# Where the last batch of a grouped convolution is normalised, and the order of the work behind the last block

## The chip, the cores and the metric

The kernel runs on one core of a Trainium2 chip. Its time is the device time of one execution in microseconds (us): 2987.53 us is the median of three runs, which lie between 2986.3 and 2987.64 us. All data are float32.

## The reference, cut to what matters

The input `x` has shape (32, 14, 14, 512). Two layers follow each other; both add their result to their own input.

```
x = x + blocks(gn(x))            # layer 0
x = x + conv3x3(gn(x), W)        # layer 1: 32 groups of 16 channels, padding SAME

def gn(v):                       # for each image and each group of 16 channels
    return (v - mean) / sqrt(var + 1e-5)

def blocks(x):
    for i in range(18):
        nx = gelu(x @ block_w[i] + block_b[i])       # 512 x 512, for every pixel
        if i in (11, 14, 17):
            pooled = nx.mean over the pixels
            h = gelu(pooled @ fc1_w[t] + fc1_b[t])
            gates = softmax((h @ fc2_w[t] + fc2_b[t]).reshape(-1, 3, 512), axis=1)
            nx = nx + gammas[t] * (gates * anchors).sum()
        x = nx                                       # blocks 1, 4 and 9 are the anchors
    return x
```

What matters here is the second layer: a mean and a scale for each image and group have to be known before the convolution of that image can run on normalised data, while the addition at the end takes the data as they were.

## The kernel before, in words

**Pairs and blocks.** The 32 images are worked on in 8 pairs p of two tiles n, each tile with two images (392 pixels). Channels lie on the partitions, in four chunks c of 128. One `block` is one of the 18 multiplications for one pair, done by Strassen's scheme in seven products of eight matmuls (L390). There are 144 blocks and one empty step (GAP), 145 steps in an order written out in `steps`; the blocks of neighbouring pairs are interleaved.

**Ticks.** All other work is put into a calendar: seven ticks belong to each block, and `block` calls `run(tick)` after each product (after the copies or additions that belong to it). What stands in a tick is issued then, in the order in which it was put there, and each engine works through its own instructions in that order. `at` puts a function at a fixed tick; `put` looks for the first tick from a given one on that has room for its costs (`ROOM`, in us for VectorE as "dve" and ScalarE as "act"), and takes the room away; `hold` only takes room away. From `tend` = 7 x 145 = 1015 on there are no blocks, the room of a tick is `TAIL`, and the ticks give nothing but an order. In the text "tick +4" is `tend` + 4.

**Input.** `plan_start` loads each later pair's input in eight pieces of 98 pixels (`load_in`, L245, three buffers of `inpool`), turns each by four transposes (`turn_in`, L258), takes statistics and normalises, within the 35 ticks ahead of the pair's first block.

**End of a pair.** After block 17 `plan_head` and `plan_gates` issue the gates: `gate_hidden` (hps, L506), `gate_logits` (lps, L522), `gate_softmax`, and then for each chunk `gate_part` (L580), `gate_last` (L594, ScalarE) and `gate_add` (L602). A DMA of the POOL queue (`residual`, L666) adds layer 0's input to the result. `plan_norm` takes statistics (L196), brings them to scales (`scales_mean`, `scales_rstd`, `scales_newton`, the first two with a matmul, L203, that adds up the 16 partitions of a group), and writes each chunk to DRAM twice with `columns`: as it is (e=0, a copy by ScalarE, L680) and normalised (e=1, L692 by ScalarE, for the last pair L690 by VectorE). The DMAs are those of L699, two of 224 KB for each copy, in the tensor `x2d`.

**Convolution.** Two pairs make a batch m of 8 images, of which there are four. A batch has 16 units u, four for each chunk; a unit has two groups g. `unit_load` brings both copies (e=0 and e=1) into a tile `xs` by one DMA of 448 KB (L817) and, where they are not held, the weights as bands. In `xs` a partition holds one channel and column of the image, so the eight groups of a chunk lie side by side along the tile's free dimension, and no longer on partitions of their own. `unit_taps` runs 12 matmuls on e=1 (cps, L838), `unit_sum` adds the result to e=0 (L848), `unit_out` transposes (tpo, L862), copies (L867) and, after the fourth unit of a chunk, stores (L872). Batches 0 to 2 run beside the blocks of later pairs; the last six units of batch 2 and all of batch 3 (pairs 6 and 7) run behind the last block. PSUM has six buffers for products and units, and two for everything that is called `aux` (hps, lps, tpo, tpi, mps, vps).

**Start.** While the first scales are computed, 20 matmuls of constant data (`warm`, L950) run on TensorE. `load_gates` brings the gates' weights (L476, L481) at the block's tick 4.

Of the kernel before, what the change touches and what calls it, by code (L numbers as in the profile page):

```python
# [19 lines left out]
def kernel(  # L20
# [21 lines left out]
    P = 128  # L42
# [28 lines left out]
    fpool = ctx.enter_context(tc.tile_pool(name="fpool", bufs=1))  # L71
    qpool = ctx.enter_context(tc.tile_pool(name="qpool", bufs=38))
    tmp = ctx.enter_context(tc.tile_pool(name="tmp", bufs=6))
    inpool = ctx.enter_context(tc.tile_pool(name="inpool", bufs=3))
    outpool = ctx.enter_context(tc.tile_pool(name="outpool", bufs=2))
    cvpool = ctx.enter_context(tc.tile_pool(name="cvpool", bufs=2))
    small = ctx.enter_context(tc.tile_pool(name="small", bufs=2))
# [31 lines left out]


    ROOM = {"dve": (1.7, 0.0, 3.4, 3.4, 1.7, 0.0, 0.0), "act": (1.0, 0.8, 1.5, 1.5, 1.0, 0.8, 0.8)}
    TAIL = {"dve": 3.0, "act": 3.6}
    left = {e: {} for e in ROOM}

    def at(tick, fn, *args):
# [42 lines left out]
        mask[:, 1 : GP + 1], ident.rearrange("p (i k) -> p k i", k=GP), AX.X, ALU.add  # L158
    )

    mhalf = const.tile([P, NR], F32, name="mhalf")
    nc.vector.memset(mhalf, -0.5)

# [131 lines left out]
    def plan_start(p):  # L295

        t0 = NP7 * at_step[p, 0]
        parts = [(2 * p + n, s) for n in range(2) for s in range(TS)]
        NIN = 3
        a = t0 - LEAD  # L300
        turned = []
        for j, (t, s) in enumerate(parts):
            at(t0 - LEAD - 6 if j < NIN else turned[j - NIN], load_in, t, s)
            turned.append(put(max(a, turned[j - NIN] + 4 if j >= NIN else 0), {"act": 0.6}, turn_in, t, s))
            a = turned[j] + 1
        b = 0
        for n in range(2):
            for c in range(NCK):
                b = max(b, put(
                    turned[n * TS + TS - 1] + 1, {"dve": 1.0}, stats_in, 2 * p + n, c  # L310
                ))
        b = put(b + 1, {"dve": 0.8}, lambda: scales_mean(pst[p]))
        b = put(b + 1, {"dve": 0.2}, lambda: scales_rstd(pst[p]))
        b = put(b + 2, {"dve": 0.8}, lambda: scales_newton(pst[p]))
        e = b
        for c in range(NCK):
            e = max(e, put(b, {"dve": 1.6}, norm_in, p, c))
        b = e

        assert b < t0  # L320
        at(t0 - 1, take_start, p)
# [290 lines left out]
    def plan_head(p, i):  # L612

        k = at_step[p, i]
        t1 = NP7 * (k + 1)
        name = f"{p}_{i}"
        ti = TARGETS.index(i)
        box = boxes[p, i] = {}
        end = k == len(steps) - 1
        if p == 0:  # L620
            at(t1 + 1, gate_differences, k, ti)
        at(t1 + (0 if end else 1), gate_hidden, k, ti, name, box)
        box["base"] = {
            (h, n): put(t1, {"dve": 1.0}, gate_base, p, i, h, n) for h in range(2) for n in range(2)
        }
        a = t1 + (1 if end else 2)
        while room("dve", a) < 2.2:
            a += 1
        at(a, gate_logits, k, name, box)
        return put(a, {"dve": 2.2}, gate_softmax, ti, name, box)  # L630
# [40 lines left out]
    def columns(p, c, n, d, e, images=range(NI)):  # L671


        nx = boxes[p, NB - 1]["nx"]
        if n == 0 and 0 in images:
            d[e, c] = qpool.tile([P, W, PV], F32, tag="q", name=f"xc{e}_{p}_{c}")
        xc = d[e, c]
        src = nx[c // NH][n][:, c % NH, :].rearrange("p (b w h) -> p w b h", w=W, h=H)
        if e == 0:
            nc.scalar.copy(  # L680
                xc[:, :, n * NI * H : (n + 1) * NI * H].rearrange("p w (b h) -> p w b h", h=H), src
            )
        else:
            for b in images:
                q0 = (n * NI + b) * H
                r = c * NB4 + n * NI + b
                o, i = xc[:, :, q0 : q0 + H], src[:, :, b]
                scale, bias = d["mr"][:, 1, r : r + 1], d["mr"][:, 2, r : r + 1]
                if p == NPAIR - 1:
                    nc.vector.tensor_scalar(o, i, scale, bias, ALU.mult, ALU.add)  # L690
                else:
                    nc.scalar.activation(o, i, AF.Identity, scale=scale, bias=bias)  # L692
        if n == 0 or NI - 1 not in images:
            return
        del d[e, c]
        m, j = divmod(p, BP)
        for v in range(2):
            w0 = v * (W - KC)
            nc.sync.dma_start(  # L699
                x2d[m][c].rearrange("(q k) e v n -> q k e v n", k=KC)[  # L700
                    :, :, e, v, j * PV : (j + 1) * PV
                ],
                xc[:, w0 : w0 + KC],
            )

    def plan_norm(p, d, a, chunks):

        def stats(n, c, b):  # L710
            if "st" not in d:
                d.update(stats_tiles(f"b{p}"))
            stats_of(d, boxes[p, NB - 1]["nx"][c // NH][n][:, c % NH], c, n, (b,))

        last = a
        for c in chunks:
            for n in range(2):
                for b in range(NI):
                    last = max(last, put(a, {"dve": 0.36}, stats, n, c, b))
        r = chunks[0] * NB4, (chunks[-1] + 1) * NB4  # L720
        b = put(last + 1, {"dve": 0.8}, lambda: scales_mean(d, *r))
        b = put(b + 1, {"dve": 0.2}, lambda: scales_rstd(d, *r))
        b = put(b + 2, {"dve": 0.8}, lambda: scales_newton(d, *r))
        b += 1
        for c in chunks:
            for n in range(2):
                a = put(a, {"act": 0.6}, columns, p, c, n, d, 0)
        out = []
        for c in chunks:
            for n in range(2):  # L730
                for i in range(NI):
                    need = {"dve": 0.4} if p == NPAIR - 1 else {"act": 0.5}
                    b = put(b, need, columns, p, c, n, d, 1, (i,))
            out.append(b)
        return out

    def plan_end(p):
# [75 lines left out]
    def unit_load(m, u):  # L813

        c, ul = divmod(u, UC)
        xs = cvpool.tile([P, 2, 2, 2 * NV], F32, tag="x", name=f"x_{m}_{u}", bufs=NX)
        nc.sync.dma_start(  # L817
            xs.rearrange("r g e n -> r g (e n)"),
            x2d[m][c].rearrange("(g r) e v n -> r g (e v n)", r=P)[:, 2 * ul : 2 * ul + 2],
        )  # L820
        if u in bands:
            bw = bands[u] if m < NBAT - 1 else bands.pop(u)
        else:
# [2 lines left out]
                bw.rearrange("p g y d -> p (g y d)"), band[u].rearrange("p g n -> p (g n)")  # L826
            )
        units[m, u] = {"xs": xs, "bw": bw}

    def unit_taps(m, u):  # L830
        d = units[m, u]
# [46 lines left out]

    done = []

    def plan_unit(m, u, tk, ahead, stay=False):
        b = tk - ahead
        if not stay and len(done) >= NBW:
            b = max(b, done[-NBW][0])
        if len(done) >= NX:
            b = max(b, done[-NX][1])
        at(b, unit_load, m, u)
        a = max(b + 2, tk)
        while room("dve", a + 1) < 0.65:
            a += 1  # L890
        at(a, unit_taps, m, u)
        b = put(a + 1, {"dve": 0.65}, unit_sum, m, u)
        b = put(b + 1, {"act": 0.9}, unit_out, m, u)
        done.append((a, b))

    def plan_batch(m):


        ready = [max(ended[p][c] for p in range(m * BP, (m + 1) * BP)) for c in range(NCK)]
        if m < NBAT - 1:  # L900
            t0 = ready[-1] + 6
            t1 = ended[(m + 2) * BP - 1][-1] if m < NBAT - 2 else NP7 * at_step[NPAIR - 1, GAP] - 9
            early = NU - (NLATE + NGAP if m == NBAT - 2 else 0)
            for u in range(early):
                plan_unit(m, u, t0 + (t1 - t0) * u // early, 8)
            if m == NBAT - 2:
# [5 lines left out]
                        at(tk - 10, load_bands, (early + j,))  # L912
                    plan_unit(m, early + j, tk, 10, j >= NBW)
                for j in range(NLATE):
                    left["dve"][tend + 1 + j] += 0.65
                    left["act"][tend + 2 + j] += 0.9
                    at(tend - 12 + j, load_bands, (early + NGAP + j,))
                    plan_unit(m, early + NGAP + j, tend + j, 12, True)
        else:
            at(tend - 7, load_bands, (0, 1), wpool, "w", [P, NCK, C])  # L920
            for j in range(2):
# [1 line left out]
            at(tend + 1, load_bands, (4, 5), wpool, "w", [P, NCK, C])  # L923
            tk = 0
            for u in range(NU):
                tk = max(tk + 1, ready[u // UC] + 3, tend + NLATE)
                plan_unit(m, u, tk, 3, True)


    for s in range(TS):  # L930
# [15 lines left out]
    turn_biases(brow)  # L946

    warm = aux("warm")
    for j in range(20):
        nc.tensor.matmul(warm[:, :P], lhsT=ident, rhs=gmask, start=True, stop=True)  # L950
    scales_newton(pst[0])
    for c in range(NCK):
# [8 lines left out]
    for k in range(len(steps)):  # L961
# [9 lines left out]
            if p == 0:  # L971
                left["dve"][NP7 * (k - 1) + 4] = 0.0
        if i in TARGETS:
            at(NP7 * k + 4, load_gates, k)
            for tk, us in enumerate((0.8, 0.0, 1.5, 1.5, 0.5, 0.0, 0.0)):
                left["act"][NP7 * k + tk] = us
    for j in range(NLATE):
        left["dve"][tend + 1 + j] = TAIL["dve"] - 0.65
        left["act"][tend + 2 + j] = TAIL["act"] - 1.05
    for j in range(NLATE):  # L980
        left["dve"][tend + 1 + j] = TAIL["dve"] - 0.65
        left["act"][tend + 2 + j] = TAIL["act"] - 0.9
    left["act"][tend] = left["act"][tend + 1] = 0.0
    for j in range(NGAP):
        tk = NP7 * at_step[NPAIR - 1, GAP] + NP7 * j // NGAP
        hold("dve", tk + 1, 0.65)
# [15 lines left out]
    for g in range(C // CG):  # L1002
# [2 lines left out]
            b += 3  # L1005
        for dx in range(3):
            b = put(b, {"dve": 1.15 if dx else 0.6}, build_band, g, dx)
    assert b < ended[1][0]
    for m in range(NBAT):
        plan_batch(m)  # L1010
    for k in range(len(steps)):
# [35 lines left out]
```

## Time and profile before

The profiled execution took 2990.11 us; its span, from the first instruction to the last, is 2988.3 us. TensorE is at work in 2945.5 us of it and VectorE in 1734.0 us.

| stretch of the span | us | what runs |
|---|---|---|
| 0 to 22.04 | 22.0 | input, statistics and scales of pair 0, warm matmuls |
| 22.04 to 2882.06 | 2860.0 | the 144 blocks, with all else beside them |
| 2882.06 to 2926.0 | 43.9 | gates of pair 7, six units of batch 2, scales of pair 7 |
| 2926.0 to 2936.22 | 10.2 | TensorE without work |
| 2936.22 to 2981.26 | 45.0 | the 16 units of batch 3 |
| 2981.26 to 2988.3 | 7.0 | last copies and the last store |

The page's second part divides the span into 40 slices of 74.7 us; the rows of its chain of waits say what the end was waiting for at each moment, and the rows of an engine's waits what ended its idle time. In the rows of windows the columns are the stretch, its length, the busy time of TensorE, its weight load, VectorE, ScalarE and POOL with the number of instructions, and then the granted clock of TensorE (1.00 is full, 0.50 half), the share of the DMA engines and what they moved in GB/s.

### The profile page before, as it was taken

The page shows a single profiled execution, that of the slowest core. Times are in us where ns is not written, and L with a number is a line of the kernel's source. Part 1 is how long each engine was busy: PE and PEld are TensorE (multiplying, and loading weights), DVE is VectorE, ACT ScalarE, POOL GpSimd, SP SyncE. Part 2 cuts the span into 40 slices and gives each one's busy share as a digit, 9 for nine tenths or more (in the row PEclk, how much of TensorE's full clock was granted, in tenths as well). Part 3 has the DMA queues.
Part 4 walks back from the last instruction along what each step waited for, and adds up shares of the span by engine and source line. Part 5 has one row for each costly group of instructions (what it writes and reads, how often), then busy time and mean ns, then how long its engine had stood idle before and what let it go on. Part 6 is the DMA issues. An engine that isn't in the chain of part 4 may idle for free.

```text
span 2988.3 us, 31804 instructions
## 1 busy us (share of the span) xinstructions
PE 2945.5 (99%) x10113; PEld 1812.9 (61%) x10113; DVE 1734.0 (58%) x3309; ACT 1457.6 (49%) x3467; POOL 77.8 (3%) x60
## 2 busy tenths in 40 slices
PE   8999999999999999999999999999999999999986
PEld 5555555555566566666666666666666665656666
DVE  6877786655467454673546635565455653545663
ACT  4445445545455444554545544445445554544551
POOL 0000000000000000000000000000000000000010
PEclk9999999999999999999999999999999999999997
DMA  4444436633365345553455544555445653343678
GB/s 159 154 165 139 162 125 191 178 115 116 126 195 156 129 142 162 185 159 132 146 164 174 173 133 133 173 166 173 139 132 168 173 161 121 124 135 118 206 220 210
DMA packets 385743, 465.36 MB, mean 156 GB/s; under 512 B 150715, under 2 KB 213290, under 8 KB 385578
## 3 DMA queue, kind: packets, MB, share of 16 engines
q1 hardware_dynamic: 355178, 436.85, 46.4%
q0 software_dynamic: 4608, 12.85, 2.5%
q10 hardware_dynamic: 25792, 13.65, 1.7%
q8 instruction: 81, 1.33, 0.2%
q14 instruction: 84, 0.69, 0.1%
HBM read 381.48 MB, written 81.79 MB: 155 GB/s over the span
## 4 chain that ended last, share of the span: by engine, by line
PE 98%; DMA 1%; DVE 1%; issue 0%; ACT 0%; SPq 0%; DVEq 0%
PE x L390 51%; PE z L390 25%; PE y L390 13%; PE cps L838 5%; PE lps L522 1%; PE tpo L862 1%; PE tpi L258 1%; PE hps L506 1%; DMA tw<-in_L_conv_W_dram 0%; DMA w<-in_L_conv_fc_w_dram 0%; PE warm L950 0%; DMA w<-in_L_conv_block_w_dram 0%; DMA x2d<-xc 0%; PE mps_b L203 0%; DMA x<-x2d 0%
## 5 line engine op out<-in xcount | busy, mean ns | idle before, releaser
L390 PE MATMUL x<-t,s 128*128 128x392 f32 x2304 | 810.0, 494 | 0.0
L403 ACT ACTIVATE o<-c,bias 128x392 f32<-128x392 f32 x720 | 440.7, 620 | 663.0 <-DVE c L427 658.3
L390 PEld LDWEIGHTS x<-t,s 128*128 128x128 f32 x2304 | 432.5, 190 | 297.5
L427 DVE TENSOR_TENSOR c<-x,c 128x392 f32<-128x392 f32 x288 | 160.8, 565 | 515.5 <-PE x L390 423.8
L423 ACT COPY c<-x 128x392 f32<-128x392 f32 x576 | 278.4, 483 | 352.6 <-PE x L390 347.7
L390 PE MATMUL x<-t,w 128*128 128x392 f32 x1152 | 403.1, 493 | 0.9 <-DVE c L427 0.9
L390 PE MATMUL z<-t,s 128*128 128x392 f32 x1152 | 403.1, 493 | 0.0
L390 PE MATMUL z<-o,s 128*128 128x392 f32 x1088 | 380.9, 493 | 0.0
L390 PE MATMUL y<-o,w 128*128 128x392 f32 x1088 | 380.5, 492 | 0.0
L390 PE MATMUL x<-o,w 128*128 128x392 f32 x1088 | 380.3, 492 | 0.0
L427 DVE TENSOR_TENSOR c<-y,c 128x392 f32<-128x392 f32 x288 | 162.9, 566 | 294.3 <-PE y L390 206.7
L390 PEld LDWEIGHTS x<-t,w 128*128 128x128 f32 x1152 | 217.8, 190 | 157.9 <-DVE c L427 1.5
L390 PEld LDWEIGHTS z<-t,s 128*128 128x128 f32 x1152 | 217.0, 190 | 152.2
L369 DVE TENSOR_TENSOR t<-o,o 128x784 f32<-128x784 f32 x272 | 264.1, 971 | 65.4 <-ACT o L403 63.5
L390 PEld LDWEIGHTS x<-o,w 128*128 128x128 f32 x1088 | 206.4, 190 | 147.2
L390 PEld LDWEIGHTS y<-o,w 128*128 128x128 f32 x1088 | 205.1, 190 | 145.6
L390 PEld LDWEIGHTS z<-o,s 128*128 128x128 f32 x1088 | 205.0, 190 | 145.3
L369 DVE TENSOR_TENSOR t<-o,t 128x784 f32<-128x784 f32 x272 | 264.2, 971 | 4.7
L423 ACT COPY c<-z 128x392 f32<-128x392 f32 x288 | 139.2, 483 | 206.3 <-PE z L390 206.2
L427 DVE TENSOR_TENSOR c<-z,c 128x392 f32<-128x392 f32 x288 | 159.1, 563 | 118.8 <-PE z L390 118.0
L410 ACT ACTIVATE o<-c,bias 128x196 f32<-128x196 f32 x288 | 129.4, 450 | 91.0 <-DVE c L427 90.2
L403 ACT ACTIVATE o<-x,bias 128x392 f32<-128x392 f32 x240 | 137.5, 582 | 72.8 <-PE x L390 67.0
(107 smaller groups left out, 2061.2 us busy)
## 6 DMA issues: line engine op xcount, KB each, us to landing
w<-in_L_conv_block_w_dram SPq DMA_DIRECT2D x144, 1024.0 KB
s<-skeep SPq DMA_DIRECT2D x504, 256.0 KB
x2d<-xc SPq DMA_DIRECT2D x128, 224.0 KB
x<-x2d SPq DMA_DIRECT2D x64, 448.0 KB
skeep<-s SPq DMA_DIRECT2D x72, 256.0 KB
bw<-band SPq DMA_DIRECT2D x38, 384.0 KB
xkeep<-xt SPq DMA_DIRECT2D x32, 392.0 KB
o<-xkeep POOLq DMA_DIRECT2D x32, 392.0 KB, 7.6
```

The costliest lines, as they stand in the source:

```text
L258: nc.tensor.transpose(tp[:, c * TP : (c + 1) * TP], xs[:, c * P : (c + 1) * P], ident[:TP, :TP])
L369: nc.vector.tensor_tensor(t[j], i0, i1, ALU.subtract)
L390: nc.tensor.matmul(acc[d][:, :N], lhsT=lhsT[:, kk, d * P : (d + 1) * P], rhs=rhs[:, kk, :], start=first and kk == 0, stop=kk == NH - 1, sk ...
L403: nc.scalar.activation(o[:, d, :], srcs[d], AF.Gelu_apprx_tanh, bias=bias[:, r : r + 1])
L410: nc.scalar.activation(o[:, d, sl], srcs[d][:, sl], AF.Gelu_apprx_tanh, bias=bias[:, r : r + 1], accum_out=pooled[:, c, m : m + 1],)
L423: nc.scalar.copy(cs[d], acc[d][:, :N])
L427: nc.vector.tensor_tensor(cs[d], acc[d][:, :N], cs[d], ALU.add)
L506: nc.tensor.matmul(hps[:, :NB4], lhsT=w1[:, kk, :], rhs=box["pooled"][:, kk, :], start=(kk == 0), stop=(kk == NCK - 1),)
L522: nc.tensor.matmul(lps[:, m * NB4 : (m + 1) * NB4], lhsT=w2[:, m * P : (m + 1) * P], rhs=h, start=True, stop=True,)
L838: nc.tensor.matmul(pv[:, :, lo:hi], lhsT=d["bw"][:, g, dy], rhs=xv[:, :, lo + dy - 1 : hi + dy - 1], start=j == 0, stop=j == 2, skip_group ...
L862: nc.tensor.transpose(tp[:NV, j * P : (j + 1) * P], d["xs"][:, g, 0, v * NV : (v + 1) * NV], ident)
```

## The change

1. For pairs 6 and 7 `plan_norm` no longer calls `columns` with e=1. In its place a new function, `spread_scales`, multiplies the chunk's means and scales by a mask, so that each partition keeps its own group's value in its own column, and adds up over all partitions by a matmul with a matrix of ones (`ones`, new); ScalarE copies the result to the tile `spread`. Every partition then has the values of all eight groups of the chunk.
2. `unit_load` brings only e=0 for batch 3 (224 KB), and the new `unit_norm` makes e=1 from it in `xs`: for each of the two groups a subtraction and a multiplication on VectorE.
3. The units behind the last block get fixed ticks (`fixed`): taps two ticks apart, the sum one tick after the taps, the transposes three ticks after them, which is behind the next unit's taps. In batch 3 `unit_norm` stands one tick ahead of its taps, which is the tick of the sum of the unit before; `plan_unit` puts it there after that sum.
4. The last gates' steps have fixed ticks as well (logits +1, softmax +3, gates from +4 on); `scales_mean`, `scales_rstd` and `scales_newton` of all pairs are no longer moved to a tick with room, and the copies of e=1 of pairs 0 to 5 follow earlier. `TAIL` falls to 1.5 and 1.7.
5. `load_gates` of the last block moves from the block's tick 4 to its tick 1.
6. `inpool` has two buffers in place of three; a piece of the input is loaded when the piece two before it is turned, and turned at least three ticks later (before: three pieces and four ticks).
7. 16 warm matmuls in place of 20.

```diff
+    ones = const.tile([P, P], F32, name="ones")
+    nc.vector.memset(ones, 1.0)
...
-        NIN = 3
+        NIN = 2
...
-            turned.append(put(max(a, turned[j - NIN] + 4 if j >= NIN else 0), {"act": 0.6}, turn_in, t, s))
+            turned.append(put(max(a, turned[j - NIN] + 3 if j >= NIN else 0), {"act": 0.6}, turn_in, t, s))
...
+        if end:
+            at(t1 + 1, gate_logits, k, name, box)
+            at(t1 + 3, gate_softmax, ti, name, box)
+            return t1 + 4
...
+    spread = const.tile([P, NCK, GP, 2, BI], F32, name="spread")
+
+    def spread_scales(p, c, d):
+        shape = [P, GP, 2, NB4]
+        own = small.tile(shape, F32, tag="own", name=f"own_{p}_{c}")
+        nc.vector.tensor_tensor(
+            own, d["mr"][:, 0:2, c * NB4 : (c + 1) * NB4].unsqueeze(1).to_broadcast(shape),
+            ident[:, ::CG].unsqueeze(2).unsqueeze(3).to_broadcast(shape), ALU.mult,
+        )
+        ps = aux(f"sps_{p}_{c}")
+        n = GP * 2 * NB4
+        nc.tensor.matmul(
+            ps[:, :n], lhsT=ones, rhs=own.rearrange("p g v b -> p (g v b)"), start=True, stop=True
+        )
+        j = p % BP
+        nc.scalar.copy(
+            spread[:, c, :, :, j * NB4 : (j + 1) * NB4],
+            ps[:, :n].rearrange("p (g v b) -> p g v b", v=2, b=NB4),
+        )
...
+        b = last + 1
+        for us, fn, step in (
+            (0.8, scales_mean, 1), (0.2, scales_rstd, 2), (0.8, scales_newton, 1)
+        ):
+            hold("dve", b, us)
+            at(b, fn, d, *r)
+            b += step
+        late = p >= NPAIR - BP
...
+            if late:
+                b = put(b, {"dve": 0.2, "act": 0.25}, spread_scales, p, c, d)
+                out.append((a, b))
...
+        ne = 4 * NV if m < NBAT - 1 else 2 * NV
+        nc.sync.dma_start(xs.rearrange("r g e n -> r g (e n)")[:, :, :ne], src[:, :, :ne])
...
+    def unit_norm(m, u):
+        xs = units[m, u]["xs"]
+        c, ul = divmod(u, UC)
+        shape = [P, 2, BI, H]
+        for g in range(2):
+            o, i = [xs[:, g, e].rearrange("p (v b h) -> p v b h", v=2, h=H) for e in (1, 0)]
+            for v, op in ((0, ALU.subtract), (1, ALU.mult)):
+                w = spread[:, c, 2 * ul + g, v].unsqueeze(1).unsqueeze(3).to_broadcast(shape)
+                nc.vector.tensor_tensor(o, i if v == 0 else o, w, op)
...
+        if fixed:
+            b = a + 3
+            if m == NBAT - 1:
+                at(a - 1, unit_norm, m, u)
+            at(a + 1, unit_sum, m, u)
+            at(b, unit_out, m, u)
...
-                    plan_unit(m, early + NGAP + j, tend + j, 12, True)
+                    plan_unit(m, early + NGAP + j, tend + 2 * j, 12 + j, True, True)
...
-                tk = max(tk + 1, ready[u // UC] + 3, tend + NLATE)
-                plan_unit(m, u, tk, 3, True)
+                a, b = ready[u // UC]
+                tk = max(tk + 2, a + 4, b + 2, tend + 2 * NLATE)
+                plan_unit(m, u, tk, min(6, tk - a - 1), True, True)
...
-    for j in range(20):
+    for j in range(16):
...
-            at(NP7 * k + 4, load_gates, k)
+            at(NP7 * k + (1 if k == len(steps) - 1 else 4), load_gates, k)
```

More of the change, by code (lines that the diff above doesn't have):

```diff
@@ L73 @@
     tmp = ctx.enter_context(tc.tile_pool(name="tmp", bufs=6))
-    inpool = ctx.enter_context(tc.tile_pool(name="inpool", bufs=3))
+    inpool = ctx.enter_context(tc.tile_pool(name="inpool", bufs=2))
     outpool = ctx.enter_context(tc.tile_pool(name="outpool", bufs=2))
@@ L111 @@
     ROOM = {"dve": (1.7, 0.0, 3.4, 3.4, 1.7, 0.0, 0.0), "act": (1.0, 0.8, 1.5, 1.5, 1.0, 0.8, 0.8)}
-    TAIL = {"dve": 3.0, "act": 3.6}
+    TAIL = {"dve": 1.5, "act": 1.7}
     left = {e: {} for e in ROOM}
@@ L625, in plan_head @@
         }
-        a = t1 + (1 if end else 2)
+        if end:
+            at(t1 + 1, gate_logits, k, name, box)
+            at(t1 + 3, gate_softmax, ti, name, box)
+            return t1 + 4
+        a = t1 + 2
         while room("dve", a) < 2.2:
@@ L688, in columns @@
                 scale, bias = d["mr"][:, 1, r : r + 1], d["mr"][:, 2, r : r + 1]
[L689 to L692, printed above, removed]
+                nc.scalar.activation(o, i, AF.Identity, scale=scale, bias=bias)
         if n == 0 or NI - 1 not in images:
@@ L720, in plan_norm @@
         r = chunks[0] * NB4, (chunks[-1] + 1) * NB4
[L721 to L724, printed above, removed]
+        b = last + 1
[6 more added lines that the diff above has]
+        late = p >= NPAIR - BP
+        out = []
         for c in chunks:
@@ L727, in plan_norm @@
                 a = put(a, {"act": 0.6}, columns, p, c, n, d, 0)
-        out = []
-        for c in chunks:
+            if late:
+                b = put(b, {"dve": 0.2, "act": 0.25}, spread_scales, p, c, d)
+                out.append((a, b))
+        for c in chunks if not late else ():
             for n in range(2):
                 for i in range(NI):
-                    need = {"dve": 0.4} if p == NPAIR - 1 else {"act": 0.5}
-                    b = put(b, need, columns, p, c, n, d, 1, (i,))
-            out.append(b)
+                    b = put(b, {"act": 0.5}, columns, p, c, n, d, 1, (i,))
+            out.append((a, b))
         return out
@@ L816, in unit_load @@
         xs = cvpool.tile([P, 2, 2, 2 * NV], F32, tag="x", name=f"x_{m}_{u}", bufs=NX)
[L817 to L820, printed above, removed]
+        src = x2d[m][c].rearrange("(g r) e v n -> r g (e v n)", r=P)[:, 2 * ul : 2 * ul + 2]
+        ne = 4 * NV if m < NBAT - 1 else 2 * NV
+        nc.sync.dma_start(xs.rearrange("r g e n -> r g (e n)")[:, :, :ne], src[:, :, :ne])
         if u in bands:
@@ L879, with plan_unit @@
     done = []
-    def plan_unit(m, u, tk, ahead, stay=False):
+    def plan_unit(m, u, tk, ahead, stay=False, fixed=False):
         b = tk - ahead
@@ L888, in plan_unit @@
         a = max(b + 2, tk)
-        while room("dve", a + 1) < 0.65:
+        while not fixed and room("dve", a + 1) < 0.65:
             a += 1
         at(a, unit_taps, m, u)
-        b = put(a + 1, {"dve": 0.65}, unit_sum, m, u)
-        b = put(b + 1, {"act": 0.9}, unit_out, m, u)
+        if fixed:
[4 more added lines that the diff above has]
+            at(b, unit_out, m, u)
+        else:
+            b = put(a + 1, {"dve": 0.65}, unit_sum, m, u)
+            b = put(b + 1, {"act": 0.9}, unit_out, m, u)
         done.append((a, b))
     def plan_batch(m):
-        ready = [max(ended[p][c] for p in range(m * BP, (m + 1) * BP)) for c in range(NCK)]
+        ready = [
+            [max(ended[p][c][v] for p in range(m * BP, (m + 1) * BP)) for v in range(2)]
+            for c in range(NCK)
+        ]
         if m < NBAT - 1:
-            t0 = ready[-1] + 6
-            t1 = ended[(m + 2) * BP - 1][-1] if m < NBAT - 2 else NP7 * at_step[NPAIR - 1, GAP] - 9
+            t0 = ready[-1][1] + 6
+            t1 = ended[(m + 2) * BP - 1][-1][1] if m < NBAT - 2 else NP7 * at_step[NPAIR - 1, GAP] - 9
             early = NU - (NLATE + NGAP if m == NBAT - 2 else 0)
@@ L914, in plan_batch @@
                 for j in range(NLATE):
-                    left["dve"][tend + 1 + j] += 0.65
-                    left["act"][tend + 2 + j] += 0.9
                     at(tend - 12 + j, load_bands, (early + NGAP + j,))
-                    plan_unit(m, early + NGAP + j, tend + j, 12, True)
+                    plan_unit(m, early + NGAP + j, tend + 2 * j, 12 + j, True, True)
         else:
@@ L977 @@
     for j in range(NLATE):
[L978 to L983, printed above, removed]
+        hold("dve", tend + 2 * j + 1, 0.65)
+        hold("act", tend + 2 * j + 3, 0.9)
+    hold("dve", tend, -0.6)
+    hold("dve", tend + 1, -0.3)
+    hold("dve", tend + 3, 0.85)
+    for tick in range(tend, tend + 4):
+        hold("act", tick, room("act", tick))
     for j in range(NGAP):
@@ L1007 @@
             b = put(b, {"dve": 1.15 if dx else 0.6}, build_band, g, dx)
-    assert b < ended[1][0]
+    assert b < ended[1][0][1]
     for m in range(NBAT):
```

## The prediction

> **What bounds the kernel now.** The page first, then TensorE's waits: where it works without a break, only what adds to TensorE's own work can cost, and where it waits, the change can win.
>
> ```profile
> span 2988.3 us, 31804 instructions
> PE 2945.5 (99%) x10113; PEld 1812.9 (61%) x10113; DVE 1734.0 (58%) x3309; ACT 1457.6 (49%) x3467; POOL 77.8 (3%) x60
> ...
> PE cps L838 <- DMA x<-x2d: 10.2, 1, 10.2
> PE hps L506 <- DMA w<-in_L_conv_fc_w_dram: 5.5, 1, 5.5
> ...
> PE mps_b L203 <- DVE e_b L227: 3.5, 1, 3.5
> PE vps_b L203 <- DVE dv_b L216: 3.1, 2, 2.1
> ```
>
> All of these but 4.3 us of first input and one wait of 0.9 us near 56 us lie behind 2882.06, where the last block ends. The blocks are bound by TensorE, the tail of 106.2 us by what TensorE waits for. The chain of waits shows the largest gap and the last units:
>
> ```profile
> 2927.23 5.11 DMA x2d<-xc
> 2932.36 0.04 issue
> 2932.41 3.77 DMA x<-x2d
> 2936.17 0.04 issue
> 2936.22 4.57 PE cps L838 x12
> ...
> 2941.12 2.27 PE cps L838 x12
> ...
> 2977.66 2.18 PE cps L838 x12
> 2979.87 0.63 DVE x L848
> 2980.50 0.14 issue
> 2980.63 0.63 PE tpo L862 x4
> ```
>
> Normalised data go to DRAM (5.11) and come back (3.77); then come 16 units at 2.17 + 0.44 = 2.61 us (taps, transposes), of which the first is cold (4.57). From the last tap to the end of the span it is 8.5 us, before and after.
>
> **Start.** In the rows of `warm` the matmuls are at full speed from about 18.6 on, with some 11.5 passes in a us. Four matmuls fewer are 8 passes, 0.70 us. The first product then waits some 0.1 for VectorE's first four normalising steps (L284: 2.43 for 8 from 20.38, so until 21.63). Gain **0.6**. Bounds 0 and 0.7.
>
> **The blocks.** TensorE's work stays; the question is new waits.
> - Input with two buffers: at 515 to 525 us a piece was issued at 519.78 behind 1024 KB of weights and two stores of 392 KB; the windows there move all these bytes by 523.5. By the new ticks that place in SP's queue holds a piece turned after the third product, near 526.5: 3 us to spare. For pair 1 the piece is issued at 170.52 behind 1.5 MB moving at 350 GB/s, has landed by 174 and is turned at 175.3. I take 0. Bounds: 0, and 2 us for each of 7 pairs, 14.
> - Scales at fixed ticks: `scales_mean` comes two ticks earlier, behind the y product; VectorE's statistics end at 538.5 there, y at 540.8. `put` keeps finding room for all other VectorE work, and the moved tap loads (4 ticks ahead of their use in place of 5; 16 issues took 6.25 us) cost VectorE about 1 us, while a stall of 7.4 us cost TensorE 0.9. 0; bounds 0 and 1.
>
> **The tail up to the first unit of batch 3**, on the clock of this trace. `load_gates` moves in SP's queue ahead of the four stores of 2875.5 to 2880.8, so to about 2876; its weights came 5.2 us after their issue, so they are there by 2883.1, when pooled is (L410 ends at 2883.0). The stores behind it are needed 30 us later. hps 0.79, taps 2.17, lps 1.70, softmax 2.6 (as from 2897.28): the gates are ready at **2890.4**, before at 2899.96. Now something else is late: `residual`.
>
> ```profile
> L666 POOL DMA_DIRECT2D o<-xkeep x4: 844/921/997, 2881.6 to 2885.3; - x4
> DMA to landing us min/median/max: 6.2/9.9/11.8
> ```
>
> `gate_part` needs it. `scales_newton` of pair 6 (1.0 us) now stands ahead of `gate_base`, so the first two are issued near 2882.2 and 2883.1; with 9.9 the third `gate_part` starts at 2893.0 (bounds 2890.4 and 2895). Queued behind it on VectorE is the product of `spread_scales` for pair 6, and behind that one's matmul on TensorE the taps of unit 12: taps at 2893.8, a gap of almost 4 us since unit 11, with four transposes in it. Units 12 to 15 take 4 x 2.17 + 3 x 0.44 + 0.7 for mean and variance + 0.5 of handovers = 11.2, until 2905.0, cold taps and transposes 2.9 more: 2907.9. VectorE then works off 4.4 us (sum, newton 1.0, an addition, five statistics and parts, three products of `spread_scales`), until 2912.3. The e=0 columns are stored from 2904.3; with 5.1 to land and 3 for half the load (estimate from 3.77) they are there at 2912.5. **First taps at 2913.5**, 22.7 us before 2936.2. So the 10.2 us wait is gone, and 3.6 MB of stores and as much loading with it.
>
> **The 16 units.** `unit_norm` has no row. Its nearest is a multiplication with a repeated operand:
>
> ```profile
> L787 DVE TENSOR_TENSOR bt<-tw,mask x96: 541/552/560, 53.8 to 462.2; 128x384 f32<-128x384 f32 x96
> ```
>
> For 784 and 392 elements without repeats the next one starts after 0.89 and 0.48, which is 1.05 ns per element; 384 repeated fit that line. 224 elements: next start after 0.30, end after 0.385, a dependent one after 0.415. Four make 1.44. That VectorE has 2.0 us a unit and TensorE 2.61 hides nothing: in their tick the sum of unit u stands first and waits for the taps of u, the norm of u+1 comes behind it, and the taps of u+1 wait for that. Whether they wait for both groups is seen from two instructions that write one tile:
>
> ```profile
> 2808.92 0.81 ACT L594 ACTIVATE gq<-o,g 128x196 f32<-128x196 f32 x2
> ...
> 2809.76 0.57 DVE L602 TENSOR_TENSOR o<-o,gq 128x392 f32<-128x392 f32 x1 [2.11 <-ACT gq L594]
> ```
>
> ScalarE goes on with the other half of gq; the addition starts after its own two. So the taps wait for the first group alone: 0.03 + sum 0.53 + 0.415 + 0.385 + 0.14 = 1.50 behind the last tap, and with 2.17 a unit takes **3.67** in place of 2.61. Six of the 15 steps carry more VectorE work in between. The second: variance 0.35, its step 0.1, three parts 1.0, sum 0.53, norm 1.44, addition 0.48, statistics 0.54, product 0.2, handover 0.14, spreading 0.2, taps 2.17: 7.15. The next five, added up in the same way, 4.7, 5.2, 4.1, 4.7 and 4.7. Sum 30.5 + 9 x 3.67 = **63.5** from last tap to last tap.
>
> [...] Row first:
>
> ```profile
> 2882.00:2886.00 4.00, 0.06 (x1) 1.00 1.05 205
> 2886.00:2890.00 4.00, 2.47 (x10) 0.50 1.04 301
> ...
> 2938.00:2942.00 4.00, 4.00 (x19) 0.68 1.19 292
> ```
>
> The columns are TensorE's busy time, then its clock. After less than 4 us without work the clock is at half; from 2936.22 it takes 4.4 us of taps without a break to return (0.68 is 64% at half). [...] So unit 12, the first unit of batch 3 (6 us behind unit 15) and the second (5 us behind the first, waiting as listed) are cold. [...] I take the row: 2.4 more. [...]
>
> **The sum.** First taps 2913.5, cold 4.57: 2918.1; 63.5: 2981.6; two cold units 4.8: 2986.4; end 8.5: 2994.9; start -0.6: 2994.3, against a span of 2988.3. The execution of 2990.11 is 2.6 above the median of the runs; the difference of +6.0 is laid on the median: **2993.5**. The 22.7 us won ahead of the units are spent in them: 15 x 1.06 = 15.9 for the turn through VectorE, 7.9 for other VectorE work in it, 4.8 for the clock.
>
> **Rivals.**
> - Clock holds: units 12, the second and the third warm. -7.7: 2985.8. For it: no gap is longer than 6 us. Against it: the row of 0.50.
> - Faster: `unit_norm` lies behind the taps of the unit before, as its 2.0 against 2.61 us would allow, and the clock holds: a further 9 x 1.06 = 9.5 off, 2976.3. It decides if VectorE comes to the norm before the sum. Against it: the order inside the tick.
> - Clock stays at half: with 1.5 us of pause in each unit it doesn't return, or falls again. 13 units x 2.4 = 31 more: 3024.7; every other unit: 3009. For it: 2914 to 2926 at 0.50 with a busy share under a half. Against it: a cold unit is busy for 4.57 of 6.1 us.
> - Input late: 1 to 2 us for each of seven pairs, 3000.5 to 3007.5. Against it: 1.3 and 3 us to spare.
>
> **How the numbers follow.** Forecast 0.45 (its own range 2988 to 3001), clock holds 0.12, faster 0.13, half clock 0.22, input 0.08. A measurement tells 0.2%, 6 us, from no change; the forecast lies on that bound, 0.26 slower and 0.19 same. Slower 0.26 + 0.22 + 0.08 = 0.56; same 0.19 + 0.09; faster 0.13 + 0.03. The range 2978 to 3015 leaves out the end of the half clock and the faster end.
>
> **What would show it.** Right: the last units 3.7 us apart with TensorE waiting for VectorE (x, L848's tile); taps of 4.57 at the first units of batch 3; no wait of tpi for input. Wrong: units 2.61 apart; gates waiting for nothing at 2890; the clock at 0.50 beyond the third unit; first taps of batch 3 after 2918 or before 2909.

## The result, and the profile after

The changed kernel takes **2997.0 us**, the median of 11 runs (2994.24 to 2998.76), beside 2989.42 us for the kernel before on the same chip (11 runs, 2986.3 to 2994.88). The ratio is 1.0023, with a 95% interval from 1.0013 to 1.0032: the change costs a little. The profiled execution took 2994.24 us.

Line numbers are now those of the changed kernel, some 40 higher in the convolution: taps L878, `unit_sum` L888, `unit_norm` L868, the product of `spread_scales` L715 and its matmul L721, transposes L902, `gate_part` L582. The page of the changed kernel begins:

```profile
span 2992.5 us, 31865 instructions
PE 2950.6 (99%) x10121; PEld 1815.9 (61%) x10121; DVE 1752.8 (59%) x3366; ACT 1451.1 (48%) x3459; POOL 78.2 (3%) x60
```

VectorE has 18.8 us more work than before and TensorE 5.1; the span is 4.2 longer. TensorE's waits (total, times, longest, in us) tell which work it is that counts:

```profile
PE cps L878 <- DVE x L868: 11.6, 12, 1.0
PE sps L721 <- DVE own L715: 8.4, 6, 2.3
PE sps L721 <- DVE e_b L229: 4.5, 1, 4.5
```

The waits for x2d (10.2), for the gates' weights (5.5) are gone, and those of mps_b and vps_b (3.5 and 3.1) are no longer among the long ones. In their place stand twelve waits of about 1 us for `unit_norm`, and waits for the spreading of scales. Where this puts the end is seen in four stretches (us, from the starts and ends of TensorE's rows):

| stretch | before | after | difference |
|---|---|---|---|
| to the end of the blocks | 2882.06 | 2880.96 | -1.1 |
| end of the blocks to the first taps of batch 3 | 54.2 | 27.9 | -26.3 |
| first taps of batch 3 to the end of the last taps | 43.6 | 75.2 | +31.6 |
| last taps to the end of the span | 8.5 | 8.4 | -0.1 |

So the tail begins 26 us sooner and is 32 us slower. The chain of waits (start, duration) shows the steady turn of the last units, and further up what held the first unit behind the gates:

```profile
2882.30 8.30 DMA o<-xkeep
...
2890.63 0.04 DVE o L582
...
2890.97 0.23 DVE own L715
...
2891.34 0.41 PE sps L721 x2
...
2954.55 2.44 PE cps L878 x12
2957.02 0.62 DVE x L888
2957.64 0.31 DVE x L868
2957.97 0.40 DVE x L868
2958.42 2.44 PE cps L878 x12
```

In the last five rows TensorE and VectorE work strictly in turn: taps, sum, two operations of the norm of the first group, the next taps. From one taps to the next it is 3.87 us; before it was 2.60. TensorE's timeline shows the first four units of batch 3:

```profile
2908.85 4.61 PE L878 MATMUL cps<-x,bq 128*128 128x224 f32 x12
...
2919.03 4.58 PE L878 MATMUL cps<-x,bq 128*128 128x224 f32 x12
...
2926.25 2.38 PE L878 MATMUL cps<-x,bq 128*128 128x224 f32 x12
...
2931.43 4.10 PE L878 MATMUL cps<-x,bq 128*128 128x224 f32 x12 [0.98 <-DVE x L868]
```

The same twelve matmuls take 2.4 us or 4.1 to 4.6. The windows say why for the first of them (the column ahead of the DMA share and the GB/s is TensorE's granted clock):

```profile
2908.00:2912.00 4.00, 4.00 (x14) 3.81 (x14) 1.94 (x8) 0.74 (x2) 0.00 (x0) 0.50 1.01 258
2960.00:2964.00 4.00, 2.99 (x18) 2.71 (x17) 2.01 (x5) 0.59 (x2) 0.00 (x0) 1.00 0.85 231
```

At the first unit the clock is halved; in the steady loop, with TensorE at work in 2.99 of 4 us, it stays full. The second unit runs at 0.50 as well (window 2919 to 2923), and so does the fourth (2931.5 to 2933.5); the third runs at 1.00 (2926 to 2928.5).

### The profile page after: what moved, and what is told of

The parts are those of the page before. It is cut to its first block, busy times and chain, and to the rows that moved or that the text cites. A ratio compares the mean times of both kernels' runs of the same rounds, so it can differ in the third digit from the quotient of the medians.

```text
span 2992.5 us, 31865 instructions
## 1 busy us (share of the span) xinstructions
PE 2950.6 (99%) x10121; PEld 1815.9 (61%) x10121; DVE 1752.8 (59%) x3366; ACT 1451.1 (48%) x3459; POOL 78.2 (3%) x60
```

## The experiments

All ratios are to the kernel before, run beside it on the same chip, with 95% intervals. The chips are not the same in all rows, so ratios are compared across rows, and medians only between runs of one chip (e1 to e4; e5 to e7; e8 to e10).

| run | base | median us | ratio |
|---|---|---|---|
| e1 norm ahead of the sum | after | 2979.31 | 0.9966 (0.9954 to 0.9979) |
| e2 no norm | after | 2973.49 | 0.9950 (0.9936 to 0.9963) |
| e3 extra matmuls | after | 2992.00 | 1.0007 (0.9999 to 1.0016) |
| e4 gates' weights early | before | 2989.49 | 1.0000 (0.9992 to 1.0008) |
| e5 gates' weights late | after | 2997.28 | 1.0027 (1.0017 to 1.0037) |
| e6 e1, pair 6 spread early | e1 | 2973.30 | 0.9946 (0.9933 to 0.9958) |
| e7 start and input alone | before | 2988.23 | 0.9999 (0.9990 to 1.0007) |
| e8 e6 with extra matmuls | e6 | 2969.76 | 0.9942 (0.9928 to 0.9955) |
| e9 pair 7 spread later | e6 | 2972.37 | 0.9949 (0.9937 to 0.9962) |
| e10 e9 with extra matmuls | e9 | 2971.19 | 0.9946 (0.9934 to 0.9959) |
| e11 scales placed by room | after | 2996.58 | 1.0027 (1.0016 to 1.0037) |

**The order inside the tick (e1).**

```diff
-                at(a - 1, unit_norm, m, u)
+                at(a - 2, unit_norm, m, u)
```

> Changed kernel with one edit: the norm of unit u+1 is issued one tick earlier, so that on VectorE it stands ahead of the sum of unit u. Theory (it is the order inside the tick that makes the taps wait for VectorE, not VectorE's amount): units that were 3.87 us apart come to 2.6 to 2.7 apart, set by TensorE's taps 2.17 and transposes 0.44; nine such steps at the end and a part of the six before them gain 12 to 18 us, so about 2979 to 2985 us, below the kernel before. Rival A (VectorE's amount with its handovers sets the turn): nothing moves by more than 2 us, 2995 to 2999. Rival B (the clock falls in another place): units as in the theory, but one or two more of them at 4.1 to 4.6 us, so 2 to 5 us less gain.

The theory held: from 1.0023 to 0.9966, some 17 us, by one digit. The timeline of e1, TensorE and VectorE together:

```profile
2948.45 0.62 DVE L888 TENSOR_TENSOR x<-x,cps 128x448 f32<-128x448 f32 x1 [0.52 <-PE cps L878]
...
2948.68 2.33 PE L878 MATMUL cps<-x,bq 128*128 128x224 f32 x12
...
2948.99 1.54 DVE L868 TENSOR_TENSOR x<-x,spread 128x224 f32<-128x224 f32 x4
...
2951.29 2.33 PE L878 MATMUL cps<-x,bq 128*128 128x224 f32 x12
```

The norm runs while the taps of another unit do, and the taps come 2.60 or 2.61 us apart, as before the change. VectorE's amount per unit is the same as in the changed kernel. From the first taps to the end of the last it is 55.9 us in place of 75.2; 4.5 of these 19.3 us are lost again ahead of the first taps (2913.31 in place of 2908.85): unit 12 of batch 2 ran there at half clock (4.58 us), and the norm of unit 0 now stands on VectorE ahead of a product of `spread_scales` (1.45 us). Rival A is refuted.

**Without the norm (e2).** The taps of batch 3 read the columns as they were loaded, so the convolution of the last batch is made of data that are not normalised.

```diff
-            xv = d["xs"][:, g, 1].rearrange("p (b h) -> p b h", h=H)
+            xv = d["xs"][:, g, 1 if m < NBAT - 1 else 0].rearrange("p (b h) -> p b h", h=H)
...
-            if m == NBAT - 1:
-                at(a - 1, unit_norm, m, u)
```

> Changed kernel without unit_norm: the convolution of batch 3 is made of data that are not normalised (its taps read the columns as loaded); spread_scales stays. Theory: four operations of together 1.54 us leave VectorE's chain in each unit, the taps of u+1 wait for nothing but their own unit's transposes, units come 2.6 apart, the first ones as soon as their input is loaded: 15 x 1.26 = 19 us less between first and last tap, 2976 to 2981 us. Rival (the turn through VectorE is carried by the sum and the evacuation of the partial sums, not by the norm): units stay above 3.3 us, 2990 or more.

The last units again come 2.60 us apart, just as with the norm in e1: once it stands ahead of the sum, the norm costs the steady loop nothing. Outside that loop it still costs something: the runs of e2 (2971.48 to 2976.63 us) lie below those of e1 on the same chip (2977.49 to 2979.53), and from the first taps to the end of the last it is 53.9 us in place of 55.9. How much of the 5.8 us between the medians is the norm stays open, since the ratios' intervals overlap and in the profiles e2 is only 2.8 us shorter.

**The clock (e3).** Extra matmuls of constant data keep TensorE at work in its waits.

```diff
+    for tick, n in ((tend + 12, 10), (tend + 13, 2), (tend + 14, 2), (tend + 17, 22), (tend + 19, 9), (tend + 21, 4)):
+        at(tick, fill, n)
```

`fill` is n matmuls of `ident` with `gmask`, 128x128, into a PSUM buffer of its own.

> Changed kernel with 49 extra 128x128 matmuls of no use in the waits of TensorE ahead of unit 12's sums and the first five units of batch 3. Theory (pauses of TensorE halve its clock and cost 2.2 us at each of the three cold units, 4.61, 4.58 and 4.10 us against 2.4): these units come to 2.4 to 2.7, the extra matmuls delay the path by 1 to 2, net 3 to 6 us less, 2991 to 2994. Rival (those units are slow for another reason, or matmuls this short don't hold the clock): the same three rows at 4.1 to 4.6, time equal or up to 3 us longer, 2997 to 3000.

In the windows of e3 the clock is full in the stretches where it was at half:

```profile
2908.00:2912.00 4.00, 3.93 (x34) 3.65 (x33) 3.90 (x16) 1.79 (x6) 0.00 (x0) 1.00 0.69 187
2920.00:2924.00 4.00, 4.00 (x30) 3.96 (x30) 1.98 (x6) 0.81 (x3) 0.00 (x0) 1.00 0.84 179
```

The taps of the first, second and fourth unit take 2.41, 2.38 and 2.43 us in place of 4.61, 4.58 and 4.10. From the first taps to those of the fourth unit it is 18.0 us in place of 22.6. So these three long rows were the clock. Unit 12, which got no extra matmuls, ran at 3.51 us here, and the first taps came 3.3 us later than in the changed kernel. Of the time, 0.0016 of the ratio came back, about 5 us, with intervals that overlap by a little.

**The gates' weights alone (e4).**

```diff
-            at(NP7 * k + 4, load_gates, k)
+            at(NP7 * k + (1 if k == len(steps) - 1 else 4), load_gates, k)
```

> Kernel before with one part of the change alone: the weights of the last block's gates are asked for at tick 1 of their step in place of tick 4. Theory: the wait of 5.5 us ahead of hps goes, the gates are ready some 5 to 9 us earlier, but behind them stand the residual's accumulation into SBUF, then the store and load of the normalised columns, so that 3 to 7 us of it reach the end: 2982 to 2986 us. Rival (the other waits of the tail swallow all of it): 2988 to 2990, no difference.

The rival held. The wait of 5.5 us is gone, and hps starts at 2882.92 in place of 2887.53. TensorE's timeline of e4, with the line numbers of before, shows where it went:

```profile
2904.68 4.11 PE L838 MATMUL cps<-x,bq 128*128 128x224 f32 x12 [4.86 <-DMA x<-x2d]
...
2935.58 4.06 PE L838 MATMUL cps<-x,bq 128*128 128x224 f32 x12 [9.17 <-DMA x<-x2d]
```

The last unit of batch 2 now came sooner than its input, whose load, issued at 2894.91, took 9.73 us; and the first unit of batch 3 still waited for the normalised columns, until 2935.58 in place of 2936.22.

**The gates' weights late again (e5).** The same line of the changed kernel is set back:

```diff
-            at(NP7 * k + (1 if k == len(steps) - 1 else 4), load_gates, k)
+            at(NP7 * k + 4, load_gates, k)
```

> Changed kernel with one of its parts undone: the weights of the last block's gates are asked for at tick 4 of their step again. Theory (the same edit alone on the kernel before was worth nothing, because the store and reload of normalised columns swallowed it; with these gone the gates stand on the path again): hps starts 4 to 6 us later, gates ready near 2895 in place of 2889, the residual no longer waited for, the taps of unit 12 and the first taps of batch 3 3 to 5 us later: 3000 to 3002 us against 2997 of the changed kernel. Rival (the residual's accumulation, landing at 2890.6, hides it here too): 2996 to 2998.

TensorE's timeline of e5:

```profile
2883.11 1.03 PE L508 MATMUL hps<-pool,w 128*128 128x4 f32 x8 [2.56 <-DMA w<-in_L_conv_fc_w_dram]
...
2892.62 0.41 PE L721 MATMUL sps<-own,ones 128*128 128x64 f32 x2 [1.83 <-DVE own L715]
```

The weights landed earlier than in the profile of before (a wait of 2.6 us, not 5.5), hps came 2.3 us later than in the changed kernel, unit 12 1.3 and the first taps 1.2 later. Such an amount is within the measurement, and 1.0027 against 1.0023 does not tell e5 from the changed kernel; but 2997.28 us lies where the rival has it, and short of the theory's 3000 to 3002. In the profile the residual hides about half of the 2.3 us.

**Pair 6 out of the way (e6).**

```diff
-                b = put(b, {"dve": 0.2, "act": 0.25}, spread_scales, p, c, d)
+                if p == NPAIR - 2:
+                    b = tend + 3
+                    at(b, spread_scales, p, c, d)
+                else:
+                    b = put(b, {"dve": 0.2, "act": 0.25}, spread_scales, p, c, d)
```

> The norm ahead of the sum, as in e1, and the scales of the last but one pair are spread at tick tend+3, right behind the softmax, in place of behind the gates' sums of each chunk. Theory (the residual, landing at 2890.8, held TensorE only because this product stood behind gate_part on VectorE): unit 12's taps follow unit 11 without a wait and at full clock, unit 12's sum comes some 4 us sooner, and with it the gates' addition, the statistics and the first taps of batch 3: 4 to 7 us less than e1, 2972 to 2975 us. Rival (the chain of the last pair from the residual to its scales sets the first and second taps of batch 3, whatever TensorE did before): first taps at 2912 to 2914 as in e1, 2977 to 2980 us.

The theory held. TensorE's timeline of e6, where the lines of the convolution are 4 higher:

```profile
2890.27 2.33 PE L882 MATMUL cps<-x,bq 128*128 128x224 f32 x12
...
2907.71 4.13 PE L882 MATMUL cps<-x,bq 128*128 128x224 f32 x12
...
2918.23 0.69 PE L721 MATMUL sps<-own,ones 128*128 128x64 f32 x2 [3.33 <-DVE own L715]
2918.71 3.74 PE L882 MATMUL cps<-x,bq 128*128 128x224 f32 x12
```

Unit 12 starts at 2890.27 at full clock (in e1 at 2891.95, 4.58 long), and the first taps of batch 3 come 5.6 us sooner than in e1, at 2907.71. `gate_part` waits for the residual here too, by 0.17 us (in e1 by 1.30), but the product is no longer queued behind it. Of the 5.6 us, 2.2 are the clock of unit 12: it took 2.33 us in all four kernels with this edit (e6, e8, e9, e10), and 3.5 to 4.6 in four of the other six with the change (e1, e2, e3, e11; 2.38 in the changed kernel and in e5). The intervals of e1 and e6 still overlap by a little.

**What is left (e8, e9, e10).** The first two lines are e8, added to e6, with `fill` as in e3; the others are e9, which moves the spreading for the chunks 1 to 3 of pair 7 behind other taps. e10 has e9 and the first two groups of e8.

```diff
+    for tick, n in ((tend + 12, 8), (tend + 14, 8), (tend + 18, 14)):
+        at(tick, fill, n)
...
-                    b = put(b, {"dve": 0.2, "act": 0.25}, spread_scales, p, c, d)
+                    b = put(b + (c > 0), {"dve": 0.2, "act": 0.25}, spread_scales, p, c, d)
```

> e6 with 30 extra 128x128 matmuls of no use in three waits of TensorE: behind the transposes of unit 14, behind those of unit 15, and ahead of the second product that spreads scales. Theory (the two taps of 4.13 and 3.74 us in e6 are the halved clock alone): both come to 2.4, 2 to 3.5 us less than e6, 2970 to 2971 us. Rival (what waits on VectorE decides; a faster unit only waits longer for the next scales): rows of 2.4 us, but less than 1 us of gain.

> e6 with the spreading of the last pair's scales for the chunks 1 to 3 one tick later, so that on TensorE it stands behind the taps of unit 2, which do not need it. Theory (the wait of 3.3 us ahead of unit 2 is a matter of TensorE's queue alone): unit 2 starts some 2 us sooner, limited by its own norm, with a gap under 2.6 us and so at full clock; 2 to 4 us less than e6, 2969 to 2971 us. Rival (VectorE's work of the last pair bounds units 2 to 6 anyway): the wait moves to a later unit, within 1 us of e6, 2972 to 2974 us.

> e9 with the first two groups of extra matmuls of e8. Theory (both gains are separate): 4 to 6 us less than e6, 2967 to 2969 us. Rival (VectorE bounds units 0 to 6): no more than the better of e8 and e9.

In e8 both taps take 2.4 us, and the fourth unit starts at 2920.36 in place of 2924.13; the span is 3.8 us shorter than that of e6. The ratios, 0.9942 and 0.9946, have overlapping intervals, so that the times alone don't show the gain. In e9 unit 2 follows the first taps by 8.1 us in place of 11.0, but the wait goes to unit 3: 2.75 us for the same scales, and its taps at half clock (4.61). Unit 3 starts 15.9 us behind the first taps in e9 and 16.4 in e6: the rival, VectorE's work for the last pair, holds. e10 is no better than e8. On the one chip that ran all three, every run of e8 (2968.92 to 2970.95 us) is shorter than every run of e9 (2971.11 to 2973.48). The lowest ratio is that of e8, 0.9942.

**The start and the blocks (e7, e11).** e7 puts three parts of the change into the kernel before:

```diff
-        NIN = 3
+        NIN = 2
...
-            turned.append(put(max(a, turned[j - NIN] + 4 if j >= NIN else 0), {"act": 0.6}, turn_in, t, s))
+            turned.append(put(max(a, turned[j - NIN] + 3 if j >= NIN else 0), {"act": 0.6}, turn_in, t, s))
...
-    for j in range(20):
+    for j in range(16):
```

`inpool` has two buffers there as well. e11 puts `scales_mean`, `scales_rstd` and `scales_newton` of pairs 0 to 5 of the changed kernel back to ticks with room:

```diff
-            hold("dve", b, us)
-            at(b, fn, d, *r)
-            b += step
+            if p < NPAIR - BP:
+                b = put(b, {"dve": us}, fn, d, *r) + step
+            else:
+                hold("dve", b, us)
+                at(b, fn, d, *r)
+                b += step
```

> Kernel before with three parts of the change alone: two input buffers in place of three, pieces turned from three ticks behind in place of four, four warming matmuls fewer. Theory: the first product starts 0.2 to 0.5 us earlier, no wait of tpi for input except the first, the blocks end 0.1 to 0.5 us earlier, the time is that of before within 1 us. Rival (two buffers are too few at some pair): waits of tpi for input of 1 us or more at one of the seven pairs, 1 to 8 us longer. If the blocks end 1.2 us earlier, as in the changed kernel, it is this part that did it, and if not, it is the fixed ticks of the scales.

> Changed kernel with one part undone for pairs 0 to 5: their scales are placed where VectorE has room again, in place of at fixed ticks. Theory (the fixed ticks are what let the blocks end some 1.1 us earlier, since they bring groups of small matmuls of the scales together with others): from the first hps (253.2 in the changed kernel) to the last product of the blocks it takes 0.8 to 1.2 us longer than there, as before the change; the tail is as there; the whole is longer by about 1 us, less than a measurement tells. Rival (another part made the blocks shorter): from the first hps to the last product the same as in the changed kernel within 0.2 us.

The measure is the stretch from the first hps to the start of the last product of the blocks, which leaves the start out: before 2625.97 us, after 2624.98, e11 2625.96, e7 2626.56. The amount repeats: e4, whose blocks are those of before, has 2625.96, and seven of the eight other kernels with the fixed ticks have 2624.97 or 2624.98 (e3 2625.37). So the fixed ticks of the scales made the blocks 1.0 us shorter, and e11 gives it back. That it comes from groups of small matmuls that now stand next to each other, as the expectation of e11 has it, is not shown. In e7 no later piece of the input is waited for by more than 0.4 us, and the time doesn't change; its stretch is 0.6 longer, whose cause stays open.

## Why the prediction was right

The forecast was 2993.5 us, 0.20% over the median it was laid on; measured was 0.23% over the kernel before run beside it. Its sum against the span was 2994.3 us, and the span is 2992.5. The mechanism was right: the wait for x2d went, and the time it had won was spent in the turn through VectorE. That the sum came so near is in part luck: counted with the start, the first taps came 4 us sooner than predicted (2908.85; 2913.5 less 0.6), and from there to the end of the last taps it took 2.4 us longer (75.2; 72.9 predicted).

- **Start, 0.6.** From the first warm matmul to the first product it is 5.38 us in place of 5.89. But in the ten other kernels with 16 warm matmuls it is 5.1 to 6.3 us, in e4 with 20 it is 6.7, and the first hps lies between 251.7 and 254.3 us in the thirteen profiles; a gain of this size can't be told.
- **Blocks, no new waits.** Right: TensorE waits for input only at the start. Not foreseen was the 1.0 us of the fixed ticks (e11).
- **Gates at 2890.4, residual last.** The mechanism was right: gates at 2889.0, then `gate_part` waits for the DMA, and `spread_scales` of pair 6 behind it holds unit 12. The DMA took 8.3 us and not the median of 9.9, and the blocks ended sooner, so unit 12 came at 2891.58 in place of 2893.8.
- **Unit 12 cold, 2.9.** It did not happen in this execution: the taps took 2.38 us. In e1 and e2, where the wait ahead of them was 3.2 and 4.2 us in place of 2.3, they took 4.58. So in e1 0.9 us more of waiting stands beside taps 2.2 us longer. From these taps to the next ones it is 5.22 us in e1 and 2.65 in the changed kernel, 2.6 more, where the sum had 2.9. That it stayed warm here is luck. With the item above it makes up the early first taps.
- **The turn, 3.67.** Right in its order, 3.87 in size. From taps to sum it takes 2.47 us; the prediction had 2.17 + 0.03, the distance to TensorE's next work. The result of the last matmul comes later: in the profile before too, the taps of 2977.50 are followed by their sum at 2979.87, 2.37 us behind. The other 0.1 is the first weight load: before, it starts 0.11 us ahead of the first matmul (2977.39), now in the same moment (2954.55). The norm took 0.86 from its start to the taps, 0.94 predicted. Over nine turns the term was 1.8 us too small.
- **The loaded units.** The first six steps were 30.5 + 4.8 us for two cold units behind the first, 35.3; the ends of the taps give 35.8. In the prediction's breakdown of what is spent, the 7.9 us for other VectorE work should be 8.5: 30.5 less 6 x 3.67.
- **The clock.** Three units were cold, as many as the sum had, but not the same. That the third is cold, 2.4 of the 4.8 us in the sum, was the author's estimate: no run had shown it. Here the third was warm (2.38), and in its place the fourth was cold (4.10) behind a gap of 2.80 us. The length of the gap does not decide it: in e5 the third unit was cold (4.06) behind the same 2.64 us between the taps. What does decide it, no run shows. That pauses of TensorE make the long rows was shown by e3, where these units took 2.41, 2.38 and 2.43 us.
- **The rivals.** The clock's staying at half fell: it is 1.00 in the steady loop with pauses of 1.4 us. The rival with the norm behind the taps of the unit before was right about where the gain lies, and e1 made it so; its 9.5 us for nine turns became 11.4 (9 x 1.27), and the six loaded units and their clock gained the rest of the 19.3 us between first and last taps.
- **The prediction's own signs.** Those of being right all came: turns of 3.87 us with TensorE waiting for x, taps of 4.6 at the first units, no wait of tpi for later input. Two of those of being wrong came as well: first taps before 2909 (2908.85), and a unit at half clock beyond the third (the fourth, 4.10). They point at the two terms that were mis-sized, the work ahead of the first taps and the place of the cold units.

## What to carry to other kernels

When work is moved from a transfer to an engine in a pipelined loop, the engine's load is the smaller question; look at what stands ahead of it in that engine's queue, and on whom that waits. Here moving the same four operations from behind the sum of the unit before to ahead of it won about 17 us, and in the steady loop they then cost nothing. A wait that has gone gives its time only if nothing behind it was as late: the early weights alone were worth nothing, because two loads behind them were waited for instead.

## What was not expected of the hardware

- The last pause alone does not tell the clock. Between the end of one taps and the start of the next, pauses of 1.4 to 1.7 us were followed by taps of 2.38 to 2.43 us, and those of 3.84 us and more without extra matmuls by taps of 3.5 to 4.6 us. Between 2.5 and 3.0 us both occur: behind 2.80 us the fourth unit took 4.10 us in the changed kernel, 4.12 in e5 and 2.43 in e11; behind 2.64 us there are taps of 2.38 and, in e5, of 4.06.
- In the changed kernel the granted clock goes to half at 2907.54 us, to full at 2924.61, to half at 2931.43 and to full at 2934.85. Ahead of the third of these moments lies the pause of 2.80 us before the fourth unit of batch 3:

```profile
2928.02:2931.43 3.41, 2.05 (x17) 1.72 (x15) 2.28 (x9) 1.01 (x3) 0.00 (x0) 1.00 0.00 0
```

TensorE works in 60% of this window, and the 3.42 us behind it are at 0.50. In the steady loop, with 2.99 of 4 us (75%), the clock stays at 1.00. In e8, whose extra matmuls fill the waits, the mean granted clock over the span is 1.000, in e6 0.997. What sets the moment of a change is not shown.

- The same accumulating DMA of 392 KB (`residual`, the third of its four pieces) took 8.30 us in the changed kernel, 8.37 in e11, 9.18 in e1, 9.70 in e3 and 10.16 in e2. It landed at 2890.6 in the changed kernel and at 2890.8 in e1, where the blocks had ended 0.7 us sooner; the pause ahead of unit 12 was 3.0 and 4.1 us, and its taps 2.38 and 4.58. So about 1 us more of waiting brought 2.2 us of half clock with it.
